# A transformer block on one core: the last unit's sums on VectorE alone, inverses read per block in one transfer, three blocks divided in the projection

## The chip, the cores and the metric

The kernel runs on one core of a Trainium2 chip. The metric is device time in microseconds (us) of one execution, as the median of several runs. The core has a matrix engine (TensorE, PE in the profile; PEld is its weight load), VectorE (DVE), ScalarE (ACT), GpSimd (POOL), SyncE (SP) and 16 DMA engines that all queues share. Engines run their own instruction lists in order and wait for each other through semaphores.

## The reference

Two sequences (B = 2) of T = 2048 tokens and D = 512 channels pass one conditioned transformer block with H = 16 heads of 32 channels. Everything is float32.

```python
mod = silu(condition) @ Wada + bada
sh_a, sc_a, gt_a, sh_m, sc_m, gt_m = split(mod, 6, axis=1)
xm = layernorm(x, g1, be1) * (1.0 + sc_a) + sh_a
q, k, v = heads(xm @ Wqkv)
scores = where(causal, q @ k.T * hd ** -0.5, -inf)
x = x + gt_a * (softmax(scores) @ v @ Wproj + bproj)
xm = layernorm(x, g2, be2) * (1.0 + sc_m) + sh_m
x = x + gt_m * (gelu(xm @ W1 + b1) @ W2 + b2)
```

The softmax denominators are sums over keys, one for each query and head. They divide the attention output before the projection by Wproj.

## The kernel before, in words

**Stages.** For each sequence b: q, k and v are computed (class `Qkv`), then `attention_phase`, then `project_phase`, which forms x + gate * (attention @ Wproj + bproj) and its layernorm statistics. The projection of sequence 0 runs inside the q, k, v stage of sequence 1; that of sequence 1 runs ahead of the MLP, which closes the kernel. In the profile, "last unit 0" runs from about 750 to 811 us, "projection 0" from 811 to 876, "last unit 1" from about 1597 to 1658, "projection 1" from 1658 to 1729.

**Attention.** The work is cut into 16 units: four groups c of HC = 4 heads, and in each four blocks i of QB = 512 queries (NQ = 4). In the last group the blocks come in the order 0, 2, 1, 3 (`last_order`). A unit goes over its key tiles in steps. In a step four scores banks `st` are computed on TensorE, one for each head, ScalarE turns each into `e` = exp, and two steps later TensorE adds values times `e` into the bank `o`. The last unit has 15 steps, n_step 0 to 14; steps 12 to 14 lie on the diagonal and are masked on GpSimd (L544).

**Row sums.** In the first 12 steps of the last unit the tiles `e` of two steps are added (`pair_sums`, new tiles `ee`), then two such pairs are added (`four_sums`), and TensorE multiplies the result by ones into the bank `sm`. `add` (L564) does one addition of a 128x512 tile. It runs on GpSimd for all units except the last, where odd heads go to VectorE and even heads to GpSimd. There are 12 tiles `e` (E_BUFS), enough for three steps, and 12 tiles `ee`.

**Sums and inverses in DRAM.** `finish` stores a unit's output in `od[b][i]` and its four rows of sums in `sd[b][i]`. `load_sums` (L320) reads a block's 16 rows back spread over 128 partitions, `invert` (L326, L327) takes the reciprocals and stores them in `rd[b][i]`, and `inverses` (L334) reads them with each row repeated over its head's 32 partitions, so that tile `rb` or a reused query tile (`qst`, from `old_queries`) lines up with the block's output tile. Each such read is four transfers of 256 KB, one for each c.

**Preparation in the last unit.** `prepare(n)` runs in each step of the last unit. At n = 3 it prefetches Wproj, the outputs `at_s` of the first two blocks, x rows of the first block and of the next stage (`prefetch`). At n = 5 it inverts the sums of three blocks and scales the projection's bias and weights by the gate (L383, L390). At n = 7 it reads the inverses of the first two blocks into two query tiles (`rb_s`). At n = 9 to 12 it divides one quarter c of both blocks (L394).

**Projection.** `project_phase` goes over the four blocks in `last_order` (k = 0 to 3), each of TQ = 4 rows of 128 tokens; n counts the 16 rows. A row needs all four quarters c of its block's output. Per row: load `xt` (L917, four buffers; the first block's rows are already there), add the bias on GpSimd (L918), four matmul groups into a PSUM bank `ps_o` (six banks, shared with the transposes of the next stage's normalisation), add on VectorE (L925), statistics (L203, L204), store (L927). In rows of k = 1 and 2 one quarter of the next block is divided (L930). At row 0 the inverses of block k = 2 are requested on ScalarE's queue; at row 3 those of block k = 3, whose sums are those of the last unit.

**Order.** Instructions made through `mm` and `act` keep their program order on their engine; the planner places the others. The DMA instructions of SP and ACT share eight completion semaphores in turn, and a transfer waits until the eighth one before it has landed.

Of the kernel before, what the change touches and what calls it, by code (L numbers as in the profile page):

```python
# [8 lines left out]
F32 = mybir.dt.float32  # L9
# [3 lines left out]
ALU = mybir.AluOpType  # L13
# [4 lines left out]
P = 128  # L18
H = 16
HD = 32  # L20
EPS = 1e-5
QB = 512
# [5 lines left out]
def dit_block_kernel(  # L28
# [85 lines left out]
    for n in range(2):  # L114

        f = bp.tile([P, QB + P], F32R, tag=f"fold{n}", name=f"fold{n}")
# [7 lines left out]
    for r in (0, HD):  # L124
# [33 lines left out]
        for b in range(B)  # L158
    ]
    sd = [  # L160
        [dram.tile([C, HC, QB], F32, tag=f"s{b}{i}", name=f"s{b}{i}") for i in range(NQ)]
        for b in range(B)
    ]
    rd = [
        [dram.tile([C, HC, QB], F32, tag=f"r{b}{i}", name=f"r{b}{i}") for i in range(NQ)]
        for b in range(B)
    ]
    od = [
# [24 lines left out]
    def act(ins):  # L193

        return tc.keep_in_program_order(ins)
# [63 lines left out]
    units = []  # L259
# [4 lines left out]
    last_order = [i for _, i in units[-NQ:]]  # L264
# [8 lines left out]
    class Row:  # L273
# [43 lines left out]
        def load_sums(self, i, queue):  # L317

            r = bp.tile([P, C * HC * QB // P], F32, tag="r", name="r", bufs=3)
            queue.dma_start(  # L320
                r, sd[self.b][i].rearrange("c h (p q) -> (c h p) q", p=P // (C * HC))
            )
            return r

        def invert(self, i, r, queue):
            act(nc.vector.reciprocal(r, r))  # L326
            queue.dma_start(  # L327
                rd[self.b][i].rearrange("c h (p q) -> (c h p) q", p=P // (C * HC)), r
            )

        def inverses(self, i, rb, queue):

            for c in range(C):
                queue.dma_start(  # L334
                    rb[:, c, :],
                    rd[self.b][i][c].unsqueeze(1).to_broadcast([HC, HD, QB]),
                )

        def old_queries(self):

# [34 lines left out]
        def prepare(self, n):  # L375

            if n == 3:
                self.prefetch()
            elif n == 5:
                for k in range(3):  # L380
                    self.invert(last_order[k], self.r_s[k], nc.sync)
                self.ps_gate = rows_of(ps_sp, 0, self.b, "s")
                act(nc.vector.tensor_tensor(bgate, bgate, self.ps_gate, ALU.mult))  # L383
            elif n == 7:
                self.rb_s = [self.old_queries() for _ in range(2)]
                for k in range(2):
                    self.inverses(last_order[k], self.rb_s[k], nc.sync)
            if 5 <= n < 5 + C:
                w = self.wproj[:, n - 5, :]
                act(nc.vector.tensor_tensor(w, w, self.ps_gate, ALU.mult))  # L390
            elif 9 <= n < 9 + C:
                for k in range(2):
                    d, r = self.at_s[k][:, n - 9, :], self.rb_s[k][:, n - 9, :]
                    act(nc.vector.tensor_tensor(d, d, r, ALU.mult))  # L394

        def width(self, u, h, t, kb):
            last = kb == units[u][1]
# [95 lines left out]
    def attention_phase(row):  # L493
        b, vv, kst, qst = row.b, row.vv, row.kst, row.qst
        with pool(f"att{b}") as ap, pool(
# [64 lines left out]
                ]  # L560

            def add(u, h, dst, x, y):
                vector = u == len(units) - 1 and h % 2
                act((nc.vector if vector else nc.gpsimd).tensor_tensor(dst, x, y, ALU.add))  # L564

            def pair_sums(u, es0, es1):
                out = new_sums()
# [15 lines left out]
            def finish(u, o, sm):  # L583

                c, i = units[u]
                ot = ap.tile([P, QB], F32, tag="ot", name="ot", bufs=2)
                act(nc.scalar.copy(ot, o))
                sums = ap.tile([P, QB], F32, tag="sums", name="sums", bufs=2)
                act(nc.scalar.copy(sums, sm))
                nc.sync.dma_start(sd[b][i][c], sums[0:P:HD, :])  # L590
                nc.sync.dma_start(od[b][i][:, c, :], ot)


# [31 lines left out]
            for u, (c, i) in enumerate(units):  # L625
# [5 lines left out]
                for n_step, tiles in enumerate(steps_of[u]):  # L631
                    last = n_step == steps - 1
                    if n_step == 0:
# [4 lines left out]
                    n = row.count(  # L638
                        due(u, starts[u] + n_step) - QB // 2, u + AHEAD
                    )  # L640
# [240 lines left out]
    def project_phase(row, psum, between):  # L881

        b = row.b
        with pool(f"proj{b}") as pp:
            n = 0
            ats = list(row.at_s)
            rbs = {}  # L890
            for k, i in enumerate(last_order):
                if k in (0, 1):

                    at = pp.tile([P, C, QB], F32, tag="at", name="at", bufs=2)
                    nc.sync.dma_start(at, od[b][last_order[k + 2]])
                    ats.append(at)
                at = ats[k]
                for t in range(TQ):
                    if n in (0, TQ - 1):
                        d = 2 + n // (TQ - 1)  # L900
                        rbs[d] = (
                            row.old_queries() if d == 2
                            else pp.tile([P, C, QB], F32, tag="rb", name="rb")
                        )
                        if d == 3:
                            row.invert(
                                last_order[d],
                                row.load_sums(last_order[d], nc.scalar),
                                nc.scalar,
                            )  # L910
                        row.inverses(last_order[d], rbs[d], nc.scalar)
                    nt = b * NT + i * TQ + t
                    if k == 0:
                        xt = row.xt_s[t]
                    else:
                        xt = pp.tile([P, D], F32, tag="xt", name="xt", bufs=4)
                        nc.sync.dma_start(xt, x_rows(nt))  # L917
                    nc.gpsimd.tensor_tensor(xt, xt, bgate, ALU.add)  # L918
                    ps = psum.tile([P, D], F32, tag="mm", name="ps_o")
                    for c in range(C):  # L920
                        mm(
                            ps, at[:, c, t * P : (t + 1) * P], row.wproj[:, c, :],
                            start=(c == 0), stop=(c == C - 1),
                        )
                    nc.vector.tensor_tensor(xt, ps, xt, ALU.add)  # L925
                    stats(pp, xt, nt, mv2)
                    nc.sync.dma_start(x1d[nt], xt)  # L927
                    if k in (1, 2):
                        d = ats[k + 1][:, t, :]
                        nc.vector.tensor_tensor(d, d, rbs[k + 1][:, t, :], ALU.mult)  # L930
                    between(n)
                    n += 1
        inv_std(mv2, rstd2, b * NT, (b + 1) * NT)


    row = Row(0)
# [104 lines left out]
    first, row = row, Row(1)  # L1041
# [373 lines left out]
```

## Time and profile before

| what | value |
|---|---|
| runs of the kernel before | 2540.3, 2548.03, 2548.76 us; median 2548.03 |
| the profiled execution | 2543.34 us, of which the span from first to last instruction is 2541.5 |
| mean granted TensorE clock | 0.986 of full |
| busy: PE, DVE, ACT, POOL | 2472.5, 1359.0, 894.8, 1034.5 us |
| DMA | 277.83 MB, mean 109 GB/s |
| additions on DVE in the last unit 0 (L564) | 12 pairs and 6 fours, 25.0 us |
| additions on POOL in the last unit 0 (L564) | 12 pairs and 6 fours, 28.4 us |

Busy time is the time in which an instruction of the engine ran; "idle before" tells how long the engine stood ahead of an instruction and what released it. PEclk is the clock that TensorE was granted, 1.00 being full speed. The DMA share is the mean busy share of the 16 DMA engines.

### The profile page before, as it was taken

The page shows a single profiled execution, that of the slowest core. Times are in us where ns is not written, and L with a number is a line of the kernel's source. Part 1 is how long each engine was busy: PE and PEld are TensorE (multiplying, and loading weights), DVE is VectorE, ACT ScalarE, POOL GpSimd, SP SyncE. Part 2 cuts the span into 40 slices and gives each one's busy share as a digit, 9 for nine tenths or more (in the row PEclk, how much of TensorE's full clock was granted, in tenths as well). Part 3 has the DMA queues.
Part 4 walks back from the last instruction along what each step waited for, and adds up shares of the span by engine and source line. Part 5 has one row for each costly group of instructions (what it writes and reads, how often), then busy time and mean ns, then how long its engine had stood idle before and what let it go on. Part 6 is the DMA issues. An engine that isn't in the chain of part 4 may idle for free.

```text
span 2541.5 us, 30886 instructions
## 1 busy us (share of the span) xinstructions
PE 2472.5 (97%) x10977; PEld 1182.4 (47%) x10977; DVE 1359.0 (53%) x2780; ACT 894.8 (35%) x1667; POOL 1034.5 (41%) x1194
## 2 busy tenths in 40 slices
PE   7999999999999999999999999989999999999998
PEld 3445445454444445454544445444444444444443
DVE  3455657666556536556665757645353353344424
ACT  2213555555554012155555455503312312311310
POOL 0001786766765366168667686712101100200100
PEclk9999999999999999999999999999999999999999
DMA  6636123041203698540414112153233233322422
GB/s 220 207 120 158 38 54 81 22 109 43 93 27 120 210 298 299 178 92 22 109 43 109 38 45 75 51 193 123 83 105 121 94 99 105 111 92 72 139 83 95
DMA packets 131716, 277.83 MB, mean 109 GB/s; under 512 B 13109, under 2 KB 41821, under 8 KB 127466
## 3 DMA queue, kind: packets, MB, share of 16 engines
q1 hardware_dynamic: 123394, 248.42, 32.9%
q0 software_dynamic: 5376, 23.07, 2.5%
q10 hardware_dynamic: 2792, 4.37, 0.5%
q8 instruction: 86, 1.41, 0.2%
q14 instruction: 68, 0.56, 0.1%
HBM read 201.90 MB, written 73.92 MB: 109 GB/s over the span
## 4 chain that ended last, share of the span: by engine, by line
PE 90%; DVE 5%; DMA 4%; issue 1%; ACT 1%; POOL 0%; ACTq 0%; SPq 0%; DVEq 0%; POOLq 0%
PE st L191 19%; PE ps_y L191 15%; PE ps_h L191 15%; PE o L191 10%; PE s L191 9%; PE ps_qk L191 8%; PE sm L191 4%; PE ps_v L191 4%; PE ps_o L191 3%; DVE junk L414 1%; DMA qst<-r 1%; PE ps_xt L199 1%; DMA rb<-r 1%; DVE mx L419 1%; DMA k<-hl 1%
## 5 line engine op out<-in xcount | busy, mean ns | idle before, releaser
L538 ACT ACTIVATE e<-st 128x512 f32<-128x512 f32 (+1 forms) x1152 | 575.1, 576 | 518.6 <-PE st L191 455.6
L564 POOL TENSOR_TENSOR ee<-e 128x512 f32<-128x512 f32 x360 | 458.9, 1308 | 257.6 <-ACT e L538 256.9
L419 DVE TENSOR_REDUCE mx<-s 128x1 f32<-128x512 f32 x616 | 413.9, 687 | 269.4 <-PE s L191 268.2
L191 PE MATMUL s<-kst,qst 128*128 128x512 f32 (+3 forms) x1058 | 451.8, 445 | 11.7 <-DVE mx L414 10.2
L191 PE MATMUL st<-qst,kst 128*128 128x512 f32 (+3 forms) x1280 | 439.9, 394 | 0.0
L191 PE MATMUL o<-e,vv 128*32 128x512 f32 (+3 forms) x2560 | 296.0, 544 | 0.0
L1186 POOL TENSOR_TENSOR c<-c 128x512 f32<-128x512 f32 x32 | 40.6, 1270 | 617.6 <-DVE c L1148 586.8
L191 PE MATMUL ps_h<-sx,w 128*128 128x512 f32 x640 | 286.7, 592 | 0.0
L414 DVE CUSTOM_DVE_ANT_0 junk<-s,causal 128x384 bf16<-128x384 f32 (+3 forms) x442 | 211.3, 478 | 135.5 <-PE s L191 126.4
L191 PE MATMUL ps_y<-sh,w 128*128 128x512 f32 x640 | 279.4, 597 | 0.0
L191 PEld LDWEIGHTS st<-qst,kst 128*128 128x128 f32 x1280 | 232.1, 194 | 87.6 <-issue 63.6
L191 PEld LDWEIGHTS s<-kst,qst 128*128 128x128 f32 x1058 | 198.7, 189 | 137.2 <-issue 46.8
L544 POOL TENSOR_SCALAR_AFFINE_SELECT e<-e 128x128 f32<-128x128 f32 (+1 forms) x384 | 120.4, 331 | 338.4 <-ACT e L538 330.1
L191 PE MATMUL ps_qk<-xmT,wqkv 128*128 128x512 f32 x512 | 243.4, 604 | 2.2 <-DVE xmT L247 2.2
L564 POOL TENSOR_TENSOR ee<-ee 128x512 f32<-128x512 f32 x180 | 229.6, 1303 | 0.0
L1148 DVE TENSOR_TENSOR h<-c,ps_h 128x512 f32<-128x512 f32 x128 | 87.9, 687 | 231.9 <-PE ps_h L191 231.9
L191 PEld LDWEIGHTS ps_y<-sh,w 128*128 128x128 f32 x640 | 122.1, 192 | 149.2 <-issue 147.8
L191 PEld LDWEIGHTS ps_h<-sx,w 128*128 128x128 f32 x640 | 121.4, 190 | 150.0 <-issue 149.7
L191 PE MATMUL st<-fold,sel 32*128 32x512 f32 (+1 forms) x1152 | 166.7, 487 | 10.7 <-ACT e L538 8.3
L191 PEld LDWEIGHTS st<-fold,sel 32*128 32x128 f32 x1152 | 66.8, 184 | 197.1 <-ACT e L538 146.5
L1172 ACT ACTIVATE h<-h,cols 128x512 f32<-128x512 f32 x128 | 92.4, 722 | 182.0 <-DVE h L1148 182.0
L191 PEld LDWEIGHTS ps_qk<-xmT,wqkv 128*128 128x128 f32 x512 | 96.0, 194 | 99.5 <-issue 91.9
(125 smaller groups left out, 2377.0 us busy)
## 6 DMA issues: line engine op xcount, KB each, us to landing
qst<-q SPq DMA_DIRECT2D x128, 256.0 KB
w<-w1d SPq DMA_DIRECT2D x34, 896.0 KB
w<-w2d SPq DMA_DIRECT2D x28, 1024.0 KB
kst<-k SPq DMA_DIRECT2D x24, 1024.0 KB
q<-hl SPq DMA_DIRECT2D x32, 512.0 KB
k<-hl SPq DMA_DIRECT2D x32, 512.0 KB
kst<-k SPq DMA_DIRECT2D x32, 256.0 KB
o<-ot SPq DMA_DIRECT2D x32, 256.0 KB
```

The source lines that it names most:

```text
L191: return tc.keep_in_program_order(nc.tensor.matmul(*args, **kw))
L199: return tc.keep_in_program_order(nc.tensor.transpose(dst, src, ident[:n, :n]))
L414: nc.vector.tensor_tensor_reduce(junk[:, :w], s[:, :w], causal[:, QB - w :], 1.0, MASKED, ALU.add, ALU.max, m,)
L419: nc.vector.tensor_reduce(m, s[:, :w], axis=AX.X, op=ALU.max)
L538: act(nc.scalar.activation(e[:, :w], sts[h][:, :w], AF.Exp))
L544: nc.gpsimd.affine_select(d, d, pattern=[[0, len(tiles)], [1, P]], compare_op=ALU.is_ge, fill=0.0, base=0, channel_multiplier=-1,)
L564: act((nc.vector if vector else nc.gpsimd).tensor_tensor(dst, x, y, ALU.add))
L1148: nc.vector.tensor_tensor(dst, x, y, op)
L1172: nc.scalar.activation(d, d, AF.Gelu, bias=col(r_b1 + chunk, 1))
L1186: nc.gpsimd.tensor_tensor(c1_, c1_, c2_, ALU.subtract)
```

## The change

Four things change, for both sequences.

- In the last unit all four heads' additions run on VectorE.
- `sd` and `rd` are laid out by head first. The inverses of a block are then read in one transfer of 1 MB.
- In the last unit only the first block is divided, at n = 11 to 14, one quarter each. The second, third and fourth are divided in the projection, in the rows of the block ahead of them, and in program order.
- All requests for sums and inverses go through SP. The inverses of block k = 2 go into the query tile of the first block's inverses, so that transfer waits for that tile's last division. The fourth block's sums are loaded at row 0, inverted at row 1 and read back at row 2.

```diff
     sd = [
-        [dram.tile([C, HC, QB], F32, tag=f"s{b}{i}", name=f"s{b}{i}") for i in range(NQ)]
+        [dram.tile([HC, C, QB], F32, tag=f"s{b}{i}", name=f"s{b}{i}") for i in range(NQ)]
...
     rd = [
-        [dram.tile([C, HC, QB], F32, tag=f"r{b}{i}", name=f"r{b}{i}") for i in range(NQ)]
+        [dram.tile([HC, C, QB], F32, tag=f"r{b}{i}", name=f"r{b}{i}") for i in range(NQ)]
...
         def inverses(self, i, rb, queue):
-            for c in range(C):
-                queue.dma_start(
-                    rb[:, c, :],
-                    rd[self.b][i][c].unsqueeze(1).to_broadcast([HC, HD, QB]),
-                )
+            queue.dma_start(
+                rb, rd[self.b][i].unsqueeze(1).to_broadcast([HC, HD, C, QB])
+            )
...
-            elif 9 <= n < 9 + C:
-                for k in range(2):
-                    d, r = self.at_s[k][:, n - 9, :], self.rb_s[k][:, n - 9, :]
-                    act(nc.vector.tensor_tensor(d, d, r, ALU.mult))
+            elif 11 <= n < 11 + C:
+                d, r = self.at_s[0][:, n - 11, :], self.rb_s[0][:, n - 11, :]
+                act(nc.vector.tensor_tensor(d, d, r, ALU.mult))
...
             def add(u, h, dst, x, y):
-                vector = u == len(units) - 1 and h % 2
-                act((nc.vector if vector else nc.gpsimd).tensor_tensor(dst, x, y, ALU.add))
+                engine = nc.vector if u == len(units) - 1 else nc.gpsimd
+                act(engine.tensor_tensor(dst, x, y, ALU.add))
...
-                nc.sync.dma_start(sd[b][i][c], sums[0:P:HD, :])
+                nc.sync.dma_start(sd[b][i][:, c, :], sums[0:P:HD, :])
...
-            rbs = {}
+            rbs = {1: row.rb_s[1], 2: row.rb_s[0]}
...
-                    if n in (0, TQ - 1):
-                        d = 2 + n // (TQ - 1)
-                        rbs[d] = (
-                            row.old_queries() if d == 2
-                            else pp.tile([P, C, QB], F32, tag="rb", name="rb")
-                        )
-                        if d == 3:
-                            row.invert(
-                                last_order[d],
-                                row.load_sums(last_order[d], nc.scalar),
-                                nc.scalar,
-                            )
-                        row.inverses(last_order[d], rbs[d], nc.scalar)
+                    if n == 0:
+                        row.inverses(last_order[2], rbs[2], nc.sync)
+                        r = row.load_sums(last_order[3], nc.sync)
+                    elif n == 1:
+                        row.invert(last_order[3], r, nc.sync)
+                    elif n == 2:
+                        rbs[3] = pp.tile([P, C, QB], F32, tag="rb", name="rb")
+                        row.inverses(last_order[3], rbs[3], nc.sync)
...
-                    if k in (1, 2):
+                    if k + 1 < NQ:
                         d = ats[k + 1][:, t, :]
-                        nc.vector.tensor_tensor(d, d, rbs[k + 1][:, t, :], ALU.mult)
+                        act(
+                            nc.vector.tensor_tensor(d, d, rbs[k + 1][:, t, :], ALU.mult)
+                        )
```

`load_sums` and `invert` get the same change of index order. On SP, the order around the projection becomes: inverses of blocks k = 0, 1, 2, then output and sums of the last unit, the output of block k = 2 (`at`), the last sums (`r`), the stores of the first rows with the loads of the next stage between them, the inverses' store, the fourth block's inverses (`rb`), and only then (in projection 0) its output and the rows `xt`; in projection 1 one row `xt` stands ahead of `rb`. On VectorE, the division of block k = 2's first quarter stands behind the additions L925 of rows 4 and 5 in projection 0, and behind that of row 4 in projection 1.

More of the change, by code (lines that the diff above doesn't have):

```diff
@@ L320, in load_sums @@
             queue.dma_start(
-                r, sd[self.b][i].rearrange("c h (p q) -> (c h p) q", p=P // (C * HC))
+                r, sd[self.b][i].rearrange("h c (p q) -> (h c p) q", p=P // (C * HC))
             )
@@ L327, in invert @@
             queue.dma_start(
-                rd[self.b][i].rearrange("c h (p q) -> (c h p) q", p=P // (C * HC)), r
+                rd[self.b][i].rearrange("h c (p q) -> (h c p) q", p=P // (C * HC)), r
             )
         def inverses(self, i, rb, queue):
-            for c in range(C):
-                queue.dma_start(
-                    rb[:, c, :],
-                    rd[self.b][i][c].unsqueeze(1).to_broadcast([HC, HD, QB]),
-                )
+            queue.dma_start(
+                rb, rd[self.b][i].unsqueeze(1).to_broadcast([HC, HD, C, QB])
+            )
         def old_queries(self):
```

## The prediction

> **What bounds the kernel now.** I read the page first: TensorE is busy nearly throughout, so time can only come from its gaps.
>
> ```profile
> PE 2472.5 (97%) x10977; PEld 1182.4 (47%) x10977; DVE 1359.0 (53%) x2780; ACT 894.8 (35%) x1667; POOL 1034.5 (41%) x1194
> ```
>
> Next the busy time of each engine in four stretches (columns: stretch, length, busy us and instructions of each engine, granted clock, DMA share, GB/s): last unit and projection of each sequence.
>
> ```profile
> 755.00:812.00 57.00, 52.96 (x324) 22.46 (x323) 37.33 (x36) 30.61 (x60) 38.09 (x34) 0.91 0.17 63
> 812.00:876.00 64.00, 59.63 (x145) 27.07 (x144) 38.84 (x85) 4.02 (x7) 14.17 (x11) 0.95 0.68 233
> 1602.00:1658.00 56.00, 51.75 (x323) 21.98 (x321) 36.23 (x35) 29.81 (x59) 37.95 (x34) 0.94 0.17 64
> 1658.00:1729.00 71.00, 61.51 (x170) 29.39 (x167) 40.96 (x75) 6.64 (x11) 15.15 (x12) 0.93 0.58 186
> ```
>
> TensorE idles 4.0, 4.4, 4.3 and 9.5 us, 22 in all, and its clock is below 1.00. The timeline of TensorE shows what follows a gap: the four `st` at 797.21 take 2.26 us, against 1.08 before it.
>
> ```profile
> 785.73 1.09 PE L191 MATMUL st<-fold,sel 32*128 32x512 f32 x4
> ...
> 797.21 2.26 PE L191 MATMUL st<-fold,sel 32*128 32x512 f32 x4 [3.33 <-ACT e L538]
> ...
> 847.64 1.12 PE L199 MATMUL ps_xt<-ident,xn 128*128 128x128 f32 x4 [4.24 <-DVE xt L925]
> ```
>
> Read in windows of 2 or 3 us, the clock then stands at 0.50 for some 7 to 8 us (3.5 in the last); the busy time in it times what the clock lacks is 4.3, 3.3, 3.9 and 2.0 us. The four stages lose 8.4, 7.6, 8.2 and 11.5 us: **36 us, 1.4% of the kernel, is all that this change can touch.** The chain of waits says why:
>
> ```profile
> 773.62 12.55 DMA qst<-r
> ...
> 792.12 1.88 DVE kst L394 x3
> ...
> 830.50 7.60 DMA rb<-r
> 838.11 6.90 DMA xt<-in_x_dram
> ...
> 1676.73 16.61 DMA rb<-r
> ```
>
> In the last unit VectorE stands before a division (L394) for inverses; its additions queue behind it, ScalarE gets no tile `e`, TensorE stops. In the projections VectorE stands before L930 for `rb`, the additions L925 queue behind it, no PSUM bank comes free.
>
> **What the Trainium skill says.** "GPSIMD Engine Reference", Specifications: GpSimd's way to SBUF is shared with VectorE, with contention where a Vector instruction has two SBUF inputs. The trace agrees: the median addition on DVE takes 1746 ns with POOL adding beside it, 677 without (the minimum in the view of tile `ee`: count, ns least/median/most); on POOL 1726 against 1288 in the unit before.
>
> ```profile
> L564 POOL TENSOR_TENSOR ee<-e x12: 1269/1726/1746, 755.6 to 790.1; 128x512 f32<-128x512 f32 x12
> L564 DVE TENSOR_TENSOR ee<-e x12: 677/1746/1780, 756.1 to 794.5; 128x512 f32<-128x512 f32 x12
> ```
>
> "DMA: Bandwidth & Descriptors", Why a DMA increments its semaphore by 16 and not by 1: a transfer runs on the largest number of engines up to 16 that divides the slowest dimension of both sides. The inverses' source starts with 4 heads, so 4 engines. The trace agrees: share 0.26, 102 GB/s, with nothing else moving.
>
> ```profile
> 783.00:786.00 3.00, 3.00 (x19) 1.29 (x16) 1.21 (x1) 1.93 (x5) 3.00 (x3) 1.00 0.26 102
> ```
>
> The same page, Queues, rings and completion order: on each DMA engine a queue's descriptors are taken in order. No line of before shows it alone; I rest on it below. "TensorE: Matmul & The Clock Gate", Part 1: half clock after an idle window of about 3.4 us; the trace has it after 3.33 to 9.5 us.
>
> **The change, part by part.** T marks a projection's start.
>
> *Additions.* Off POOL: 18 per last unit. On DVE 36 x 0.64 us (spacing of two undisturbed ones, 1.28 / 2) = 23.0, against 25.0 for its 18 today. With 3 reciprocals (1.4), gate products (3.2) and 4 divisions (2.6) DVE has 30 us of work in 57. A pair of four heads takes 2.6 us of a 3.13 us step, all on one engine. POOL's four bias additions near n = 5 delay DVE by at most 4 x 1.1 us; it catches up by n = 10. The three steps of tiles `e` cover that.
>
> *Divisions in the last unit.* Requested at 771.04, five pieces of 256 KB had landed at 786.17, so a piece takes 262144 B / 102 GB/s = 2.57 us and the fixed part is 15.13 - 12.85 = 2.3. The first block's 1 MB lands at 771.04 + 2.3 + 10.3 = 783.6, and n = 11 comes at about 786: no wait. The last-unit stalls go: **-8.4 and -8.2 us.** ScalarE's four DMA issues there (0.53 us each) go too; hidden beside TensorE, counted at nothing.
>
> *Block k = 1 in the projection.* Its last quarter is divided 0.3 + 0.7 + 0.7 + 0.2 + 0.6 = 2.5 us after row 3's matmuls (wait, L925, L203, L204, L930); TensorE needs it after three quarters of row 4, 2.6 us. Nothing; a late DVE would show here at once.
>
> *Requests on SP.* Inverses of k = 2 wait for the fourth division, about 795, and land at 795 + 12.6, T + 5 where T is now 802.4. The last sums (4 rows, 4 engines) and `r` sit behind them; in projection 0 `at` waits for these sums, so `r` lands near T + 9.8 instead of by T + 8. The reciprocal stands at row 1; DVE stops about 1 us, covered by free PSUM banks. The store of inverses then waits behind 3 MB of wqkv: 4.5 MB from T + 6 at 375 GB/s, and 1.5 us to land (a store of inverses issued at 769.56 let its reader go at 771.04): about T + 19. `rb` takes 12.6 us, to T + 32. Behind it on its four engines: `at` of k = 3 (64 KB each, 2.6 us) and the rows `xt` (0.65 each), so rows 4 and 5 land at T + 35.4 and 36. Today they are issued at T + 27.2 and land at T + 34.1; similar, but today nothing of block 2 stands behind them.
>
> *The new wait.* Block 2's first division is behind L925 of rows 4 and 5: POOL 1.27 us each, then L925, L203, L925, L930: T + 39.7. TensorE has finished rows 0 to 7 and 8 transposes at 8 x 3.44 + 0.9 = T + 28.4 and stops 11.4 us. The other quarters come 2 us apart, row 8 at half clock ends at T + 47.5 instead of 31.9: projection 0 loses 15.6 instead of 7.6, **+8.0 us.** In projection 1 there is no wqkv: `rb` is issued at T + 15.6 after row 3's store and lands at T + 28.2; row 4's `xt` is ahead of it, row 5's behind it (T + 28.9). The first quarter is there, the others come at T + 33.1, 35.3 and 38.4; row 8 ends at 39.4 instead of 33.4 in steps too short to lose the clock. It loses 6 to 7.5 instead of 11.5: **-4.2.**
>
> Sum: -8.4 - 8.2 + 8.0 - 4.2 = -12.8. From the profiled execution's 2543.34 (span and 1.8 around it): **2530 us.** The median of the runs is 4.7 higher, its lowest run 3 lower. 0.5%, about what a measurement of this kernel can tell from no change, is 12.7 us.
>
> Bounds of what before does not show. A 1 MB broadcast: 10.3 us by the 102 GB/s row, up to 16.6 by the chain's `rb<-r` beside other traffic; below 10.3 only if it used more engines, which the four heads exclude. I take 10.3. DVE alone in the last unit: from no stall to the old stall (0 to 4 us each). Row loads behind `rb`: from not held up at all (the projection's old loss gone, -7.6 and -11.5) to fully behind.
>
> **Rivals.** (1) *The row loads get through.* If a ring's queue lets `xt` pass, block 2 is ready in time and nothing is given back: -8.4 - 8.2 - 4 to -7 - 8 = -28, 2515 us. For: SP issues `xt` at T + 20, seven us before today. Against: order on a queue. (2) *DVE becomes late.* Additions for four heads on one engine, the last stall comes back as ACT waiting for DVE: the gain of 16.6 falls to 8 or less, and with +8 - 4.2 it is 2539 to 2545. For: DVE is in order and divides in between; against: 30 us of work in 57. (3) *Slower.* The broadcasts on SP hold everything: each us more per MB comes twice in projection 0 (k = 2 ahead of the sums, `rb` ahead of the rows) and once or twice in projection 1. At 16.6 us per MB that is 6.3 x 4 = 25 us more: 2555. It decides from about 16.5 us per MB on. (4) The sums are the same work and the divisions the same number, so that it does nothing is only the case where both stalls shift: 2543.
>
> **How the numbers follow.** Likeliest case 0.50 (2522 to 2540 alone, 0.29 of it faster by over 0.5%), rival 1 0.27, rival 2 and 4 together 0.14, rival 3 0.09. Faster 0.29 + 0.27, rounded 0.57; same 0.34; slower 0.09. Range 2512 to 2549: down to rival 1 with a little clock, up past rival 2, leaving out most of rival 3.
>
> **What would show it.** Right: L564 on DVE near 680 ns and x36 per last unit, no TensorE gap over 1 us before L538, PEclk 1.00 there; `rb<-r` one transfer of some 12 us; in projection 0 a gap of 8 to 13 us before row 8 with releaser L930, `xt<-in_x_dram` landing after `rb`. Wrong: gaps before `st` again; rows 4 to 7 added before T + 28; `rb` faster than 9 us.

## The result, and the profile after

The changed kernel takes 2566.17 us (median of 4 runs, 2564.91 to 2568.81) against 2547.99 for the kernel before beside it (4 runs, 2540.3 to 2548.76): ratio 1.008, 95% interval 1.0058 to 1.0101. It is **slower by 20 us** by the ratio (the medians differ by 18), where 13 us less was forecast. The profiled execution took 2564.95 us, of which the span is 2563.2.

The page's line of engines shows the same work as before. TensorE's busy time has not moved. GpSimd has lost 50 us. VectorE has the additions, 36 instructions more, in the same busy time as before, since each is shorter.

```profile
PE 2471.6 (96%) x10977; PEld 1174.6 (46%) x10977; DVE 1358.3 (53%) x2816; ACT 895.2 (35%) x1667; POOL 984.7 (38%) x1158
```

So the 20 us are waits of TensorE again. Here are the four stretches, now cut at the new starts of the projections (columns as in the prediction):

```profile
745.00:803.07 58.07, 57.55 (x407) 24.67 (x407) 34.37 (x51) 34.91 (x71) 21.01 (x29) 1.00 0.16 50
803.00:893.00 90.00, 63.28 (x149) 26.88 (x146) 41.92 (x91) 4.96 (x9) 15.61 (x12) 0.85 0.62 184
1600.00:1668.00 68.00, 67.13 (x463) 28.90 (x461) 42.77 (x66) 40.73 (x83) 25.90 (x37) 1.00 0.20 62
1668.00:1752.00 84.00, 66.89 (x168) 29.55 (x165) 44.93 (x79) 6.65 (x11) 15.88 (x12) 0.86 0.56 166
```

TensorE idles 0.5 and 0.9 us in the stretches of the last units, at clock 1.00: what was meant to go is gone. In the projections it idles 27 and 17 us at clock 0.85 and 0.86: all that was won there, and more, is given back. TensorE's timeline shows where (start, length, operation, in brackets the idle time before it and its releaser):

```profile
777.78 0.49 PE L191 MATMUL st<-fold,sel 32*128 32x512 f32 x1 [0.48 <-ACT e L535]
821.20 1.13 PE L191 MATMUL ps_o<-kst 128*128 128x512 f32 x2 [3.27 <-DVE kst L924]
824.85 7.85 PE L191 MATMUL ps_o<-kst 128*128 128x512 f32 x12 [2.52 <-DVE kst L924]
858.76 5.30 PE L191 MATMUL ps_o<-kst,at 128*128 128x512 f32 x6 [18.32 <-issue]
...
1686.58 4.20 PE L191 MATMUL ps_o<-kst 128*128 128x512 f32 x4 [2.75 <-DVE kst L924]
1718.01 2.07 PE L191 MATMUL ps_o<-kst,at 128*128 128x512 f32 x2 [12.78 <-DVE at L924]
```

L924 is the division of the next block in the projection. Each row is eight matmuls, two for each quarter. The gaps at 821, 825 and 1687 lie inside row 4 (block k = 1), behind its first quarters; the texts of the experiments call them the gaps before row 4, and so it is kept below. Those at 859 and 1718 stand before row 8, the first of block 2, and behind its first quarter. Where the releaser reads `issue`, the profile shows no wait; VectorE's division of block 2's first quarter ended at 858.66, just ahead of that matmul. The chain of waits names what the divisions wait for; here are its transfers in the two projections (start, us, transfer):

```profile
803.95 10.20 DMA s<-sums
814.61 5.28 DMA r<-s
820.56 8.14 DMA r<-r
829.88 24.39 DMA xt<-in_x_dram
...
1668.99 12.29 DMA s<-sums
1681.29 2.52 DMA r<-s
1692.59 20.16 DMA xt<-in_x_dram
```

The sums are 8 KB and take 10 and 12 us. The x rows are 256 KB each, and the first of them lands 24 and 20 us after its request. On VectorE's timeline the late sums become a stop at the reciprocal, with a division of block 1 queued right behind it:

```profile
819.98 0.55 DVE L326 RECIPROCAL r<-r 128x64 f32<-128x64 f32 x1 [8.25 <-DMA r<-s]
820.45 0.12 DVE L204 BATCH_NORM_AGGREGATE mv<-stat 128x2 f32<-128x6 f32 x1
820.49 0.66 DVE L924 TENSOR_TENSOR kst<-kst,qst 128x512 f32<-128x512 f32 x1
```

And this is what the DMA engines did meanwhile. The first stretch lies in the last unit, where the prediction showed 0.26 and 102 GB/s for the kernel before; the others lie in the long gap, where no engine works at all:

```profile
781.00:784.00 3.00, 3.00 (x17) 1.15 (x17) 3.00 (x6) 2.06 (x4) 0.00 (x0) 1.00 0.26 79
...
847.00:850.00 3.00, 0.00 (x0) 0.00 (x0) 0.00 (x0) 0.00 (x0) 0.00 (x0) 0.50 0.25 68
850.00:853.00 3.00, 0.00 (x0) 0.00 (x0) 0.00 (x0) 0.00 (x0) 0.00 (x0) 0.50 0.24 94
```

A share of 0.25 is what four busy engines of sixteen give. The share is that of before, but fewer bytes move: that is the first thing that the forecast had not priced. The view of DMA traffic gives the mean rate in the stretch 776 to 790, first of before, then of after:

```profile
DMA packets 718, 1.43 MB, mean 102 GB/s; under 512 B 20, under 2 KB 20, under 8 KB 718
```

```profile
DMA packets 134, 1.06 MB, mean 76 GB/s; under 512 B 4, under 2 KB 4, under 8 KB 4
```

The packets were of 2 KB and are of 8 KB now.

By stages, with the starts of the projections taken from TensorE's timeline (first `ps_o`, then the first matmul of the next stage):

| stretch | before | after | change | forecast |
|---|---|---|---|---|
| start to projection 0 | 810.9 | 803.1 | -7.9 | -8.4 |
| projection 0 | 64.5 | 89.7 | +25.2 | +8.0 |
| to projection 1 | 782.5 | 775.3 | -7.2 | -8.2 |
| projection 1 | 70.5 | 84.0 | +13.5 | -4.2 |
| MLP | 813.0 | 811.1 | -1.9 | 0 |

The sum is +21.7, the difference of the two spans. The third stretch is long and varies by itself (below), so the last units are better read alone, on TensorE's timeline, from the transpose `ps_m` that opens them to the first `ps_o`: 66.7 us before and 58.9 after in the first sequence, 66.5 and 58.9 in the second, so -7.8 and -7.6.

### The profile page after: what moved, and what is told of

The parts are those of the page before. It is cut to its first block, busy times and chain, and to the rows that moved or that the text cites. A ratio compares the mean times of both kernels' runs of the same rounds, so it can differ in the third digit from the quotient of the medians.

```text
span 2563.2 us, 30873 instructions
## 1 busy us (share of the span) xinstructions
PE 2471.6 (96%) x10977; PEld 1174.6 (46%) x10977; DVE 1358.3 (53%) x2816; ACT 895.2 (35%) x1667; POOL 984.7 (38%) x1158
## 3 DMA queue, kind: packets, MB, share of 16 engines
q8 instruction: 86, 1.41, 0.2%
## 4 chain that ended last, share of the span: by engine, by line
PE 89%; DVE 5%; DMA 4%; issue 1%; ACT 1%; POOL 0%; SPq 0%; DVEq 0%; ACTq 0%; POOLq 0%
PE st L191 19%; PE ps_y L191 15%; PE ps_h L191 15%; PE o L191 10%; PE s L191 9%; PE ps_qk L191 8%; PE sm L191 4%; PE ps_v L191 4%; PE ps_o L191 2%; DMA xt<-in_x_dram 2%; DVE junk L411 1%; PE ps_xt L199 1%; DMA s<-sums 1%; DVE mx L416 1%; DVE ee L561 0%
## 5 line engine op out<-in xcount | busy, mean ns | idle before, releaser
L561 POOL TENSOR_TENSOR ee<-e 128x512 f32<-128x512 f32 x336 | 421.1, 1287 | 244.3 <-ACT e L535 243.8
L561 POOL TENSOR_TENSOR ee<-ee 128x512 f32<-128x512 f32 x168 | 211.0, 1285 | 0.0
```

The costliest lines, as they stand in the source:

```text
L561: act(engine.tensor_tensor(dst, x, y, ALU.add))
```

## The experiments

Theory A: the reads of inverses run on four DMA engines and are slow there; whatever else uses these engines (the last sums, `at`, the weights, the x rows, all of them split over the engines) waits for its share on these four. Theory B: the order is at fault, that of VectorE (a division ahead of an addition) or of SP's queue. All kernels in one table; P0 and P1 are the lengths of the two projections in the profiled execution, read as above. The ratio is to the kernel before, run beside each. The stretch between the projections differs by 10 us between two profiles whose last units have no long stall (782.8 with four reads, 772.6 with two), so single spans are not compared below 10 us.

| kernel | median us | ratio and 95% interval | P0 | P1 |
|---|---|---|---|---|
| after | 2566.17 | 1.008 (1.0058 to 1.0101) | 89.7 | 84.0 |
| after, four reads of 2 KB rows | 2541.28 | 0.9998 (0.9986 to 1.001) | 76.2 | 73.0 |
| after, two reads of 4 KB rows | 2548.16 | 1.0012 (1.0002 to 1.0022) | 78.0 | 74.7 |
| after, 16-row reads | 2517.59 | 0.9907 (0.9889 to 0.9925) | 66.7 | 61.7 |
| after, sums on ScalarE's queue | 2561.91 | 1.0074 (1.0056 to 1.0093) | 87.4 | 81.1 |
| after, sums and `rb` on ScalarE's queue | 2561.2 | 1.0079 (1.006 to 1.0097) | 89.9 | 80.2 |
| after, sums ahead of the third read | 2578.0 | 1.0125 (1.0102 to 1.0148) | 100.6 | 82.9 |
| after, x rows early | 2554.99 | 1.0052 (1.0034 to 1.007) | 81.5 | 77.7 |
| before, additions on VectorE only | 2536.31 | 0.9962 (0.9952 to 0.9973) | 63.7 | 72.2 |
| before, one read of 8 KB rows only | 2578.53 | 1.013 (1.0107 to 1.0153) | 67.8 | 75.8 |
| before, 16-row reads | 2516.29 | 0.9885 (0.986 to 0.991) | 64.8 | 59.1 |
| before, 16-row reads, additions on VectorE | 2518.79 | 0.991 (0.9886 to 0.9933) | 65.4 | 59.1 |
| after, 16-row reads, x rows early | 2514.85 | 0.9882 (0.9859 to 0.9906) | 60.0 | 59.9 |
| the same with 2 KB rows | 2511.92 | 0.9882 (0.9861 to 0.9903) | 60.2 | 59.1 |
| after, reads by head, x rows early | 2524.66 | 0.9917 (0.9901 to 0.9934) | 64.2 | 64.6 |

### The reads: four requests, and sixteen rows

The changed kernel with its one read split by quarters:

```diff
-            queue.dma_start(
-                rb, rd[self.b][i].unsqueeze(1).to_broadcast([HC, HD, C, QB])
-            )
+            for c in range(C):
+                queue.dma_start(
+                    rb[:, c, :],
+                    rd[self.b][i][:, c, :].unsqueeze(1).to_broadcast([HC, HD, QB]),
+                )
```

> The changed kernel with each block's inverses read in four transfers of 256 KB (rows of 2 KB), everything else in its place. Rate theory (rows of 8 KB move slower than rows of 2 KB on the four DMA engines, and all else on SP stands behind them): 1 MB takes about 10.3 us again instead of some 17, DMA at 102 GB/s with share 0.26; the last sums land 5 us sooner and the rows xt about 10 us sooner in both projections; about 2548 us, the time before. Rival, VectorE's order (the divisions in program order are the loss, whatever the transfers): unchanged, 2566 us within 3.

The loss goes, ratio 0.9998. The rate is 102 GB/s at the same share of 0.26, and the sums land in 2 us. The gaps before row 4 are gone in projection 0 (0.4 us in projection 1); before row 8 TensorE's timeline keeps this one:

```profile
845.95 5.06 PE L191 MATMUL ps_o<-kst,at 128*128 128x512 f32 x6 [14.30 <-issue]
```

Two things differ from the changed kernel here. The rate is one. The other is that the four requests for the third block go out one by one, from 786.7 to 796.3, as the divisions free each quarter of the tile, while the single request had to wait until 796.1. In the changed kernel the DMA share dips only from 0.25 to between 0.15 and 0.19 for 4 us there; so I put most of the difference down to the rate, but these runs do not split the two.

The changed kernel with the inverses stored four times, so that a read starts with 16 rows and not 4 (one request of 1 MB still, 8 KB rows still):

```diff
-dram.tile([HC, C, QB], ...)
+dram.tile([HC, 4, C, QB], ...)
...
-                rb, rd[self.b][i].unsqueeze(1).to_broadcast([HC, HD, C, QB])
+                rb,
+                rd[self.b][i].rearrange("h r c q -> (h r) c q").unsqueeze(1).to_broadcast([HC * 4, HD // 4, C, QB]),
```

> The changed kernel with the inverses stored four times, so that the read starts with 16 rows of 8 partitions each; still one transfer of 1 MB in the same place. Queue theory (a read on four DMA engines holds what follows it on SP): it spreads over 16 engines, lands in 3 to 5 us, DMA share over 0.8 while it runs, the sums land 2 to 3 us after their request and rows xt before row 8; TensorE's gaps in the projections shrink to a few us; about 2520 us. Rival, VectorE's order: gaps before rows 4 and 8 stay, over 2555 us.

25 us better than the kernel before beside it. What differs from the changed kernel is the number of engines that carry the reads; besides, each block's inverses are stored by four requests of 32 KB in place of one. A stretch of its last unit, where the changed kernel had share 0.26 and 79 GB/s:

```profile
778.00:781.00 3.00, 3.00 (x17) 1.16 (x16) 3.00 (x6) 2.06 (x4) 0.00 (x0) 1.00 0.98 221
```

VectorE's order and SP's order are those of the changed kernel, and TensorE's gaps in projection 0 fall from 26.7 us in sum to 7.1, the longest 4.59. Theory B alone is out. Nor are the stored copies the cause: the last run below reads rows that are stored once, with sixteen engines and early x rows, and its gaps in projection 0 are 4.9 us in sum. The Trainium skill, "DMA: Bandwidth & Descriptors", Rules for kernel authors, says it in advance: an outermost dimension below 16 confines a transfer to at most that many engines. The share of 0.98 agrees.

### The order of the queue

The changed kernel with the last sums' store and load, and the store of their inverses, on ScalarE's queue instead of SP's (`nc.sync` to `nc.scalar` at three places):

> The changed kernel with the last unit's sums stored, loaded and their inverses stored from ScalarE's queue instead of SP's; the reads of inverses stay on SP. Queue theory: the sums no longer stand behind the inverses of block k = 2, land within 3 to 4 us instead of 10 to 12, so the wait of the reciprocal (8.3 and 6.3 us) and TensorE's gap before row 4 go, and the rows xt, still behind rb, come about 8 us sooner; about 2548 us. Rival, VectorE's order alone: the gap before row 8 stays as long, 2560 us or more.

A miss: nothing is gained. On a queue of its own, with nothing ahead of it there, the 8 KB of sums still took, by the chain:

```profile
801.78 7.43 DMA s<-sums
```

So it was not a place in SP's queue that the sums waited for. What they share with the read on SP is the four engines.

With the read of `rb` on ScalarE's queue as well:

> As the one before, and the fourth block's inverses (rb) are read from ScalarE's queue as well. Queue theory: rows xt no longer stand behind rb on SP and share the four DMA engines with it instead; they land before row 8's turn or a few us after, so the gap before row 8 (18.3 and 12.8 us) falls under 6 us; about 2528 us. Rival, VectorE's order: the first division of block k = 2 still stands behind rows 4 and 5, gap of 8 us or more, 2545 us or more.

A miss again, 33 us off. The read `rb` no longer stands ahead of the x rows on SP, and they are still late. SP's own timeline shows their four requests stretched over 26 us, and the view of SP's waits from 800 to 860 names one cause (waiter, releaser, us in total, times, longest):

```profile
824.98 25.88 SPq L910 DMA_DIRECT2D xt<-in_x_dram  x4
```

```profile
SPq L910 <- DMA rb<-r: 18.5, 1, 18.5
```

So a request on SP stood 18.5 us for a slow transfer of the other queue. That fits the completion semaphores that the two queues share; it was not tested alone. Moving a read to the other queue thus frees neither its four engines nor, here, SP.

The two requests turned round on SP, the last sums ahead of the third block's inverses:

```diff
-                        row.inverses(last_order[2], rbs[2], nc.sync)
-                        r = row.load_sums(last_order[3], nc.sync)
+                        r = row.load_sums(last_order[3], nc.sync)
+                        row.inverses(last_order[2], rbs[2], nc.sync)
```

(with `act` around the two transfers, so that their order is kept).

> The changed kernel with one order turned round on SP: the last unit's sums are stored and loaded before the third block's inverses are requested, not after. Theory A (the sums waited for their four engines, not for the queue's or VectorE's order): s<-sums lands in about 2 us instead of 10.2, the reciprocal no longer holds the divisions of block 1, the gaps of 3.3 and 2.5 us before row 4 of projection 0 and 2.8 in projection 1 go; rb is requested some 6 us earlier but stands behind the third block's read, so most of the gap before row 8 stays: 2566 - 6 to - 12, about 2557. Rival (VectorE's order makes those gaps whatever the sums do): 2566, gaps before row 4 as they were.

Half of it came. The sums landed in 2 us and the gaps before row 4 of projection 0 are gone, so it was the third read, under way on its four engines, that had made them late. But the read went out 13 us later, and SP then stopped inside the requests for wqkv (first line, of SP's timeline); the store of the inverses and all that follows came after it (second, of TensorE's timeline):

```profile
809.92 18.62 SPq L726 DMA_DIRECT2D wqkv<-in_L_cond_Wqkv_dram  x3
```

```profile
872.45 5.24 PE L191 MATMUL ps_o<-kst,at 128*128 128x512 f32 x6 [38.84 <-issue]
```

The one gap before row 8 is 39 us where it was 18. The loss has not been removed but moved to what stands behind the read in its new place, which I had not asked: the time expected, 2557, was wrong by 21 us. Why SP stops in that request until 828.5 is not shown; until 828 the DMA share still stands at 0.24, so the read may have been under way as long. Here, then, the order on SP has a part in the loss that the four engines alone do not explain.

### The x rows

The changed kernel with x rows 4 to 7 requested at row 0, ahead of wqkv and `rb`:

```diff
+                        early = []
+                        for e in range(TQ):
+                            xt = pp.tile([P, D], F32, tag="xt", name="xt", bufs=4)
+                            nc.sync.dma_start(xt, x_rows(b * NT + last_order[1] * TQ + e))
+                            early.append(xt)
...
+                    elif k == 1:
+                        xt = early[t]
```

> The changed kernel (four engines, 8 KB rows) with the x rows 4 to 7 requested at row 0, behind the last sums and ahead of wqkv and rb. Theory A: TensorE's 18.3 us before row 8 was made of the rows' loads behind rb (rb issued at 828.8, rows landed at 854.3) and then block 2's inverses; with the rows there, block 2's first division waits for rb alone, which lands about 851: the gap shrinks by some 3 to 6 us in projection 0 and 3 to 8 in projection 1, the gaps before row 4 stay: 2566 - 6 to - 14, about 2556. Rival 1 of the prediction (rows that are not behind rb make block 2 ready in time): below 2546.

As expected: 2555. On TensorE's timeline the gap before row 8 falls from 18.3 to 5.8 us, those before row 4 stay or grow:

```profile
823.29 2.08 PE L191 MATMUL ps_o<-kst 128*128 128x512 f32 x2 [3.29 <-DVE kst L933]
829.18 7.36 PE L191 MATMUL ps_o<-kst 128*128 128x512 f32 x12 [3.82 <-DVE kst L933]
864.78 3.88 PE L191 MATMUL ps_o<-kst,at 128*128 128x512 f32 x4 [5.83 <-issue]
```

So waiting for the rows was a part of the loss, as the prediction's step had it. But rows that are requested early give back 11 us by the medians and 7 by the ratios, not the whole. The first rival, by which nothing is given back once the rows get through, does not hold for this kernel.

### The parts of the change by themselves

Before with only the additions moved:

```diff
-                vector = u == len(units) - 1 and h % 2
-                act((nc.vector if vector else nc.gpsimd).tensor_tensor(dst, x, y, ALU.add))
+                engine = nc.vector if u == len(units) - 1 else nc.gpsimd
+                act(engine.tensor_tensor(dst, x, y, ALU.add))
```

> Before with only the additions of the last unit moved to VectorE; everything else as before, the inverses in four reads of 2 KB rows. Theory A (the loss of the changed kernel is in the reads of inverses on four DMA engines): the additions fall to about 0.68 us and what they gain is kept, but the first division L394 still stands at n = 9 before inverses that need until 788, so a stall of 2 to 4 us per last unit remains; projections unchanged. 2543 - 6 to 2543 - 12: 2531 to 2537. Theory B (36 additions on one engine make VectorE late, and that is what the changed kernel pays): ScalarE's e tiles wait for VectorE, TensorE gaps in the last units at least as long as before, 2543 or more.

Measured 2536.31, 10 us less than the kernel before beside it: in theory A's band. The stall before `st` on TensorE's timeline is 1.3 us where it was 3.3, though the division still stands before its inverses:

```profile
795.42 1.96 PE L191 MATMUL st<-fold,sel 32*128 32x512 f32 x4 [1.34 <-ACT e L538]
```

Before with only the storage by head and the one read:

> Before with only the storage by head and the one-transfer read (8 KB rows, 1 MB); additions and divisions where they were. Theory A: each read runs at 61 to 90 GB/s instead of 102, so the inverses of the last unit land 5 to 8 us later behind the division at n = 9, the stall before st grows by about that much in both units, and rb lands later in the projections: 2543 + 10 to + 30, say 2560. Theory B (the layout is harmless, the loss comes from the new order of requests on SP or of VectorE): 2543, within 0.3%.

Slower by 32 us, nearly twice the 17 that I had taken: both reads of the last unit, 2 MB, are requested together and both are waited for, by the chain of waits:

```profile
771.64 27.90 DMA qst<-r
```

TensorE's timeline has a stall of 11.5 us for it where before had 3.3:

```profile
801.60 1.77 PE L191 MATMUL st<-fold,sel 32*128 32x512 f32 x3 [11.46 <-ACT e L536]
```

By itself this part costs more than the whole change. The parts do not add: the third part, which takes one of the two reads out of the last unit's divisions, hides what the second costs there and pays in the projection. On four engines with 2 KB rows the additions alone have 0.9962; with the layout, the new places of the divisions and the requests on SP it is 0.9998, and the intervals are apart. So these other parts together cost some 9 us even without the long rows; which of them does was not tested.

### What is left when the reads are on sixteen engines

Before with 16-row reads (stored by head, in one request) and nothing else:

> Before with storage by head, inverses stored four times, and one read that starts with 16 rows; additions half on GpSimd, divisions and their order as before. Theory A: a read lands in about 6 us instead of 12.6, the waits at L394 and before row 8 of the projections shrink or go; the contention of GpSimd and VectorE in the additions stays and may cost a little: 2543 - 15 to - 25, about 2522. If the changed kernel's other two parts are worth something beyond the reads, this stays 3 to 10 us above the 2517.6 of the changed kernel with 16 rows. Theory B (VectorE's order is the matter, the reads only a part): 2535 or more.

Before with 16-row reads and the additions on VectorE:

> Before with 16-row reads stored by head and the last unit's additions on VectorE alone; divisions and their place as before. Theory A (once the reads are on sixteen engines, what the additions cost in the last unit is small): the gap of 1 us before st goes, 2516 - 1 to - 5, that is 2511 to 2516. If the place of the divisions mattered by itself (the third part of the change), this would differ from the 2517.6 of the changed kernel with 16 rows by over 5 us either way.

2516.29 and 2518.79, beside 2517.59 for the whole change with 16 rows. The intervals overlap: none of the three is told from the others. With quick reads neither the additions nor the place of the divisions makes a difference that these runs can tell; a difference of 10 us would have shown, one of 3 would not.

The changed kernel with 16-row reads and the x rows early:

> The changed kernel with 16-row reads and, besides, the x rows 4 to 7 requested at row 0, right behind the last sums, so ahead of the weights wqkv and of rb. Theory A: the 4.6 us gap that the 16-row version keeps before row 8 of projection 0 is the rows' loads landing behind wqkv and rb; it goes, as do most of 2 us in projection 1: 2517.6 - 4 to - 7, about 2512. Rival (the gap comes from VectorE's order, division of block 2 behind the additions of rows 4 and 5 in any case): 2517, the gap stays above 3 us.

Measured 2514.85. The gap before row 8 is down to 1.4 us, and what TensorE's timeline still shows in projection 0 is small:

```profile
821.30 4.56 PE L191 MATMUL ps_o<-kst 128*128 128x512 f32 x10 [1.00 <-DVE kst L937]
852.25 11.43 PE L191 MATMUL ps_o<-kst,at 128*128 128x512 f32 x26 [1.39 <-DVE at L937]
```

Its interval and that of the 16-row version without early rows overlap, so the gain is seen in the trace and not told by the times.

### Row length or size of the request

The changed kernel in two reads of 512 KB with rows of 4 KB:

> The changed kernel with the inverses of a block read in two transfers of 512 KB and rows of 4 KB, still on four DMA engines. Theory A1 (the longer a row, the slower the four engines): between the 2541.3 of 2 KB rows and the 2566.2 of 8 KB rows, about 2550, and a rate between 102 and 61 to 90 GB/s. Theory A2 (a read of 1 MB in one piece is slow because of its one request, not its rows): two requests behave like four, 2541 to 2544.

The time, 2548, lies where the first theory put it; the rate does not. It is 104 GB/s in the mean between 776 and 790, as for 2 KB rows. So the rate falls between 4 and 8 KB rows, or between requests of 512 KB and 1 MB, and the 3.5 us over the four reads (by the ratios) are not clear of noise: the two intervals overlap. To part the two, the same version with early x rows and sixteen engines was run with four requests of 256 KB each, once with 2 KB rows (a loop over c around the read):

> The 16-row version with early x rows, its inverses read in four transfers of 256 KB with 2 KB rows instead of one with 8 KB rows: sixteen engines and short rows. If the row's length costs on sixteen engines as it does on four, the rate rises from 221 to 236 GB/s towards 300 or more; the time can fall little, since TensorE's gaps are 3 to 4 us in all: 2511 to 2515. If sixteen engines are limited by something else, the rate stays at 220 to 240 and the time at 2515.

and once with 8 KB rows, each request one head's, the inverses stored once:

```diff
+            for h in range(HC):
+                queue.dma_start(
+                    rb[h * HD : (h + 1) * HD],
+                    rd[self.b][i][h].unsqueeze(0).to_broadcast([HD, C, QB]),
+                )
```

> The changed kernel with early x rows and the inverses stored once, each block read in four requests of 256 KB, one for each head: a request starts with 32 partitions and its rows are 8 KB. If the number of engines follows the outermost dimension of the request, all sixteen engines carry it and the time is that of the 16-row version with early rows, 2510 to 2515; if it follows the source, which is one row, it runs on one or few engines, and the time is 2566 or more. If the 8 KB rows are what slows a read, the rate while it runs is the 221 to 236 GB/s of the one-request version; if the size of the request, it is nearer to the 285 GB/s of four requests with 2 KB rows.

Two stretches of each (columns as above), first with 2 KB rows, then with 8 KB rows:

```profile
774.00:777.00 3.00, 2.52 (x20) 0.63 (x12) 3.00 (x4) 1.50 (x3) 1.35 (x1) 1.00 0.68 215
777.00:780.00 3.00, 3.00 (x17) 1.29 (x16) 3.00 (x6) 2.06 (x4) 0.00 (x0) 1.00 0.91 279
```

```profile
774.00:777.00 3.00, 3.00 (x17) 1.16 (x13) 3.00 (x3) 1.99 (x5) 3.00 (x3) 1.00 1.03 219
777.00:780.00 3.00, 2.52 (x21) 0.77 (x20) 3.00 (x4) 1.68 (x4) 1.53 (x1) 1.00 1.00 219
```

The requests are of one size. With the longer rows the engines are busy throughout (a share above 1 can only be inexactness of the profile) and move 219 GB/s. With the shorter ones they move 215 and 279 at shares of 0.68 and 0.91, so more for the time that they are busy. Over the whole of the reads the rates are nearer: 245 GB/s at 0.80 (774 to 782) and 224 at 1.05 (773 to 781). The single request of 1 MB with 8 KB rows has 223 at 0.96 (774 to 783), like the four of 256 KB. So on sixteen engines the longer row, and not the size of the request, goes with fewer bytes per busy time. What that costs in time these runs do not tell: with early x rows, one request of 8 KB rows and four of 2 KB rows have the same ratio, 0.9882. On four engines the same was not separated; there 8 KB rows came only in requests of 1 MB. The run by head also shows that the engines follow the outermost dimension of the request: one source row repeated over 32 partitions used all sixteen. Its time stays 10 us above that of the 16-row version with early rows by the medians, though the intervals overlap slightly. On SP its reads for the third block stand between the last sums' store and load; whether that is the cause is open.

## Why the prediction was wrong

**What held.** The account of the last unit held. "The last-unit stalls go: -8.4 and -8.2 us" measured -7.8 and -7.6. VectorE does 24 additions of pairs (the line below, of the view of tile `ee`) and 12 of fours, at 686 and 685 ns in the median, and keeps up:

```profile
L561 DVE TENSOR_TENSOR ee<-e x24: 677/686/1770, 755.5 to 791.2; 128x512 f32<-128x512 f32 x24
```

The mechanism of the gap before row 8 (`rb` on four engines, rows 4 and 5 behind it, block 2's first division behind their additions) is the one found, and the second rival (VectorE late in the last unit) did not occur. That a queue's transfers are taken in order on each DMA engine, on which the forecast rested, no run here shows alone; the x rows behind `rb` landed 24 us after their request, which agrees. What failed are sizes and one wait.

**The step that failed first: "A 1 MB broadcast: 10.3 us by the 102 GB/s row [...] I take 10.3."** That row was of 2 KB pieces; the change makes them 8 KB. The first read was requested at 768.95, and its division began at 788.78 after a wait of 2.7 us: 19.8 us where 12.6 were forecast. From 769 to 789 the engines moved 1.41 MB at a mean of 70 GB/s. At that rate 1 MB is 15.0 us, and 19.8 less the fixed 2.3 is 17.5. The rest is other traffic: 0.1 MB of stores of inverses, and some of the second read, which was requested right behind the first. The bound of 16.6 did not cover it, and "below 10.3 only if it used more engines" looked on one side only. I had taken a rate and moved it to a transfer of another shape, as if it were alone on its engines.

**The second: "DVE stops about 1 us, covered by free PSUM banks."** It stopped 8.25 and 6.34 us, and "Block k = 1: Nothing; a late DVE would show here at once" is what showed, with 5.8 and 2.8 us of gaps before row 4. The sums' 10.2 us on the four busy engines were not in the working: I had queued them behind the third read and counted that read as landing at T + 5. So `r` landed at T + 16.8 in projection 0 and not at T + 9.8, `rb` was requested at T + 25.7 and not at T + 19, and row 4's x landed at T + 51.2 and not at T + 35.4. With 16 rows, or with the sums first, these gaps of projection 0 are gone or at most 1 us.

**The third: the landing of the x rows, "T + 35.4 and 36" and "T + 28.9", was too early even at the rate taken.** The version with four reads has that rate, and its projections take +11.7 and +2.5 against before, where +8.0 and -4.2 were forecast. In projection 0 `rb` was requested at T + 17.4 (T + 19 forecast), but the x rows, requested at T + 22.6, landed at T + 38.4. In projection 1 row 5's load was requested at T + 20.4 and landed at T + 33.3, where 28.9 was forecast. The last units' -15 and these +14 give the measured 0.9998. The forecast as a ratio is 2530 / 2543.34 = 0.995 and the miss 0.013, or 34 us. Some 13 of them are there with four reads too, where the projections differ from the forecast by 10 us; 21 come with the one read, by its 8 KB rows and its later start, and these two were not parted.

**The rivals.** The third was the one that happened: "The broadcasts on SP hold everything". Its price, 2555, was 11 us short; it counted what slower reads delay, and no gap in row 4. Its words also put the cause on SP's queue. For the sums, the run on ScalarE's queue shows that it is the engines; for the rest the order on SP has a part (sums first, and SP's wait for `rb`). Given 0.09, it should have had more: the trace of before already held `rb<-r` at 16.61 us. The terms written for the first rival add up to -29 to -32 us, not -28, so 2512 to 2515; nothing rests on it.

## What to carry to other kernels

In this kernel a transfer that starts with four rows takes four of sixteen DMA engines, and what needs those four meanwhile is late, from whichever of the two queues it comes: look for a DMA share of 0.25 while something waits, and give the transfer an outermost dimension of 16 or more before moving its request or its users. Here this alone, on the kernel before, brought 29 us of 2546 (ratio 0.9885), and beside it the rest of the change makes no difference that these runs can tell. When transfers are merged, the rate of the merged one has to be measured, not taken from the pieces, and what waited for the first piece now waits for the whole.

## What the runs showed of the hardware that was not expected

- On four engines, a repeated read ran at 102 GB/s with 2 KB rows, 104 with 4 KB and 76 with 8 KB (means from 776 to 790), at shares of 0.25 to 0.26. The 76 is a mean of a rate that rose from 61 to 90 in stretches of 2 us; why is not shown. On sixteen, 2 KB rows gave 245 GB/s at 0.80 and 8 KB rows 223 and 224 at 0.96 and 1.05, over the whole of two reads.
- 8 KB of sums took 7.4 us on a queue without other reads while a 1 MB read was under way on the same four engines, and 2 us where none was.
- A request on SP stood 18.5 us for a read issued on ScalarE's queue.
